# A graph layer on one core: own features one node range per pass, the neighbour product moved ahead of the sum, paced table copies, and 17 output blocks inside the last lane

## The chip, the core and the metric

The kernel runs on one core of a Trainium2 chip. The metric is the device time of one execution in microseconds. The engines are named as the profile names them: PE (TensorE, the matrix products; PEld is its weight load), DVE (VectorE), ACT (ScalarE), POOL (GpSimd) and SP (SyncE, which here only issues DMAs). Each engine runs its own queue in order; ACT and POOL issue DMAs from theirs as well.

## What is computed

There are V = 100,000 nodes with C = 64 features and E = 3.3 million edges (both directions of 1.6 million random pairs, and one loop for each node), sorted by target:

```python
h = jnp.maximum(_layernorm(x, axis=-1), 0.0)
local, nbr = h[dst], h[src]
y   = concat([local, nbr - local], -1) @ W.T + b          # per edge
s   = segment_sum(y, dst); cnt = segment_sum(1, dst)
out = x + where(cnt > 0, s / max(cnt, 1), 0)
```

The mean over a node's edges of `y` is the node's own part, `h @ (W1 - W2) + b`, plus the mean of its neighbours' `h` times `W2`. So the edge work is a sum of neighbours' rows for each target and a count.

## The kernel before

The features are padded to R = 100,352 rows, 784 for each of 128 partitions, and handled in blocks of T = 28 rows a partition, 28 blocks in all.

**Preparing** (lines 260 to 404). For each block, `center` loads x and subtracts the mean, the variance is taken from ACT's squares, and the normalized rows are split into three bf16 parts on ACT and GpSimd (L390 to L395), which are written as `h3` (L396): 3 x 64 columns and a one for the count. `own_part` turns the rows with PE (L338), adds `b` by a product of ones with three bf16 parts of `b` (L360), multiplies by `w_own` (L361) and writes `hb`. `step_own` places its units of 8 rows between the other steps.

**Sorting the first two lanes** (L1272 to L1296). Edges are cut into 384 windows of 8128, four of them to a quad, 32 quads to a lane, three lanes. A window spans fewer than 256 target nodes. `sort_lane` sorts the keys of 128 windows, one on each partition, by source: merge steps of one ACT copy (L603) and two DVE minimum and maximum operations (L597, L598), then counts that find where each of 157 source columns of 640 nodes begins (L686 on ACT, L743 on DVE). Beside it run 1400 gathers of the edges left over (`chunks`, L513), the clearing of `acc`, and 157 copies of `h3` into `tables` (L1286), one in each step from the 40th, issued by ACT.

**The lanes** (`quads`, from L939). A lane runs seven passes over its 32 quads; pass x covers the source columns from `FROM[x]` to `FROM[x + 1]` (16, five times 24, then the rest). For one column of one quad, a pick, six products of one-hot `gh` with a table column give the rows of the sources (L1102), ACT casts them (L1105), and row-tiled products over 32 rows with the one-hot `dh` add them to the quad's 4 x 256 targets in `total` (L1116). At the end of a quad's columns, `clear` adds `total` to the sums of earlier passes (L1152), which `load_sums` fetched from `part_d` (L1030), and stores them again (L1164). `whole`, the tile for that, has one buffer.

In pass 1 (`OWN`), the loops are treated apart, since their source is the target itself: `selfs` counts them (L1135, L1155), `load_sums` loads the own rows of all four windows (`own`, L1036), and `add_own` adds count times own row by eight DVE operations a quad (L1172). The store of the sums is put off until these have run.

Work in the background of the picks is called from the loop at L1310: `rest` at 0.055 a pick (`fill_lane`, which spreads a lane's sorted keys with gathers L830 and L920), and `sorting` at `SORT` = 0.135 a pick, which sorts the third lane in lane 0 and 1, but not in pass 1 and pass 6. `pinned` ties the DVE operations of such work to their place; others go when their data allow it. DMA requests on SP go in order, so a request that waits holds back the next, the loads of `srs` (L984) among them, from which `gh` is made.

In the last pass, `close` makes sums of 65 columns and `finish` stores them to `acc`; each window's last row may be shared with the next and goes to `shared`.

**The end** (from L1324). Four indirect adds bring `shared` into `acc` (L1349), flags decide whether a slow path has to run (loops with 0 turns otherwise), and 28 blocks are put out: mean of `acc` (L1431), turned (L1441), copied (L1443), multiplied by `w_mean` (L1447), added to `hb * min(cnt, 1) + x` from GpSimd (L1434, L1435, L1448) and stored (L1449).

Of the kernel before, what the change touches and what calls it, by code (L numbers as in the profile page):

```python
# [28 lines left out]
P = 128  # L29
P = 128  # L30
# [42 lines left out]
SORT = 0.135  # L73
# [10 lines left out]
SUB = 8  # L84
GP = 8
# [7 lines left out]
def rows_of(v):  # L93


    return -(-(v + 2 * P) // (P * SUB)) * P * SUB

# [14 lines left out]
def gnn_preln(ctx: ExitStack, tc, x, src_w, dst_w, src_p, dst_p, src_a, dst_a, wT, b, out, V, E):  # L112
# [45 lines left out]
    assert NE - FROM[-2] > 2 * GP and NSG > 1 and NTB - FROM[-2] // TG >= SEG // TG  # L158
# [22 lines left out]
    part_d = dram.tile([SETS, P, W, NT * CE], F32, name="part_d")  # L181
# [12 lines left out]
    w_mean = consts.tile([P, 2, C], F32, name="w_mean")  # L194
    w_own = consts.tile([P, 2, C], F32, name="w_own")
    nc.vector.memset(w_mean, 0.0)
    nc.vector.memset(w_own, 0.0)
    for i in range(2):
        nc.sync.dma_start(w_own[i * C:i * C + C, i], wT[:C])
        nc.sync.dma_start(w_mean[i * C:i * C + C, i], wT[C:])  # L200
    nc.vector.tensor_sub(w_own, w_own, w_mean)
# [9 lines left out]
    turns = consts.tile([1, 2], I32, name="turns")  # L211
# [10 lines left out]
    b3 = consts.tile([3 * 32, 2, C], BF16, name="b3")  # L222
    nc.vector.memset(b3, 0.0)
    b_part = consts.tile([P, C], BF16, name="b_part")
    for i in range(3):
        nc.vector.tensor_copy(b_part, b_sb)
        nc.vector.tensor_sub(b_sb, b_sb, b_part)
        nc.vector.tensor_copy(b3[32 * i:32 * i + 1], b_part[32 * i:32 * i + 1, None, :].to_broadcast([1, 2, C]))
    ones3 = consts.tile([3 * 32, P], BF16, name="ones3")
    nc.vector.memset(ones3, 1.0)  # L230

# [4 lines left out]
    out_v = out.rearrange("(p t) c -> p t c", p=P)  # L236
# [23 lines left out]
    with tc.tile_pool(name="pre", bufs=2) as pre, tc.tile_pool(name="small", bufs=4) as small, \  # L260
            tc.tile_pool(name="pre_ps", bufs=1, space=PSUM) as pre_ps, \
# [24 lines left out]
        def bounds(m):  # L286
            n = min(P, NCH - m * P)
            d = pre.tile([P, CHUNK], I32, name="d")
# [12 lines left out]
            l_ps = pre_ps.tile([NMT, 2, P], F32, name="l_ps")  # L301
# [29 lines left out]
        normal, made = {}, {}  # L331

        def own_part():

            def turn(t, u):
                t_ps = own_ps.tile([P, SUB // 2, P], F32, name="t_ps")
                for i in range(min(SUB, T - u) // 2):
                    nc.tensor.transpose(t_ps[:, i], normal[t][:, u + 2 * i:u + 2 * i + 2].rearrange("p a c -> p (a c)"), ident)  # L338
                return t_ps

            def finish(t, u, o_ps):
                if u == 0:
                    made[t] = pre.tile([P, T, C], F32, name="own", bufs=2)
                n = min(SUB, T - u)
                nc.scalar.copy(made[t][:, u:u + n], o_ps[:, :n])
# [5 lines left out]
            yield  # L351
            behind = None
            for at, (t, u) in enumerate(units):
# [3 lines left out]
                o_ps = own_ps.tile([P, SUB, C], F32, name="o_ps")  # L357
                o2 = o_ps.rearrange("p (i a) c -> p i (a c)", a=2)
                for i in range(n // 2):
                    nc.tensor.matmul(o2[:, i], lhsT=ones3, rhs=b3.rearrange("p a c -> p (a c)"), start=True, stop=False)  # L360
                    nc.tensor.matmul(o2[:, i], lhsT=hT[:, i], rhs=w_own.rearrange("p a c -> p (a c)"),  # L361
                                     start=False, stop=True)
                if behind is not None:
                    finish(*behind)
                if at + 1 < len(units):
                    t_ps = turn(*units[at + 1])
                behind = t, u, o_ps
                yield
            finish(*behind)
# [3 lines left out]
        def step_own(t):  # L373
            if t > 0:
                next(owns)

        center(0)
        for t in range(0, NPT, T):
            center(t + T)
            step_own(t)  # L380
# [3 lines left out]
            step_own(t)  # L384
# [3 lines left out]
            parts = pre.tile([P, T, CT], BF16, name="parts", bufs=3)  # L388
            nc.gpsimd.memset(parts[:, :, C3:], 1.0)
            nc.scalar.copy(parts[:, :, :C], xt)  # L390
            step_own(t)
# [1099 lines left out]
```

## Time and profile before

| what | us |
|---|---|
| median of 3 runs | 16983.4 (16947.2 to 16985.4) |
| profiled execution | 16993.9 |
| its span, first to last instruction | 16991.8 |
| mean granted clock of PE | 0.913 |

The page gives busy time for each engine, groups of instructions by line with count, busy time, the mean of one in ns, and the idle time ahead of them with what ended it. A windows view gives, for each stretch, its length, the busy time of PE, PEld, DVE, ACT and POOL with the number of instructions in brackets, the granted clock, the share of the 16 DMA engines in use and GB/s. A timeline gives start, length and instruction.

### The profile page before, as it was taken

What the parts mean: (1) busy time and instruction counts of PE and PEld (TensorE: products, weight loads), DVE (VectorE), ACT (ScalarE), POOL (GpSimd) and SP (SyncE); (2) the same over time, 40 slices, a digit from 0 to 9 for tenths busy, and PEclk for the clock granted to TensorE, in tenths of its full rate; (3) what the DMA queues carried; (4) which work ended last, traced back from release to release, by engine and by line L of the source; (5) the groups of instructions that cost most, each with busy time, mean ns of one, the idle gap of its engine ahead of it and who ended that gap; (6) DMA issues with size and microseconds to landing.
All of it is one profiled execution on the core that took longest, in us unless ns stands there. A gap on an engine that the chain in (4) does not pass through costs nothing. (4 is left out here: it accounts for less than half of the span.)

```text
span 16991.8 us, 762352 instructions
## 1 busy us (share of the span) xinstructions
PE 14218.4 (84%) x343411; PEld 13316.3 (78%) x343411; DVE 13850.5 (82%) x18981; ACT 8698.5 (51%) x17939; POOL 2232.9 (13%) x2043
## 2 busy tenths in 40 slices
PE   6111117999998999999999889999999989999996
PEld 5000007999997999999899889999998889999995
DVE  6787998889998889988899877779778766666784
ACT  5233346545554555565455645555554545555542
POOL 5565660000001000100000000001000000000015
PEclk7555558999999999999999999999999999999998
DMA  6962224555554455545555445555455544545557
GB/s 255 147 72 53 38 47 137 169 166 170 173 161 144 153 164 166 143 150 166 164 172 171 138 153 156 175 167 143 153 165 163 168 148 154 169 155 169 160 139 263
DMA packets 1939346, 2600.22 MB, mean 153 GB/s; under 512 B 955944, under 2 KB 1622454, under 8 KB 1931030
## 3 DMA queue, kind: packets, MB, share of 16 engines
q1 hardware_dynamic: 1765580, 2386.78, 44.6%
q0 software_dynamic: 62304, 99.25, 3.4%
q10 hardware_dynamic: 108188, 65.39, 3.0%
q8 instruction: 2684, 43.97, 1.1%
q14 instruction: 590, 4.83, 0.1%
HBM read 1898.80 MB, written 690.78 MB: 152 GB/s over the span
## 5 line engine op out<-in xcount | busy, mean ns | idle before, releaser
L1105 ACT CAST gs<-gp 128x386 bf16<-128x386 f32 x15072 | 6877.6, 486 | 5655.4 <-PE gp L1102 5234.1
L1102 PE MATMUL gp<-tab,gh 128*128 128x193 bf16 x90432 | 8118.3, 248 | 205.8 <-ACT gs L1105 110.2
L1102 PEld LDWEIGHTS <-gh 128*128 128x128 bf16 x90432 | 7612.0, 98 | 565.7 <-issue 526.4
L1116 PE MATMUL total<-gs,dh 32*128 32x193 bf16 x241152 | 5538.2, 243 | 297.2 <-issue 235.2
L1050 DVE TENSOR_SCALAR gh<-srs,pcols 128x2048 bf16<-128x2048 int16 (+1 forms) x5760 | 3954.5, 739 | 2155.6 <-PE gp L1102 1901.8
L1116 PEld LDWEIGHTS <-dh 32*128 32x128 bf16 x248832 | 5120.6, 93 | 744.8 <-issue 664.6
L470 DVE TENSOR_TENSOR dh<-dt,column 128x2048 bf16<-128x2048 int16 (+1 forms) x3840 | 4503.9, 1199 | 159.7 <-remote 97.5
L603 ACT COPY tmp<-keys 128x512 f32<-128x512 f32 (+16 forms) x1347 | 1092.0, 813 | 1852.8 <-DVE keys L598 974.7
L522 PE MATMUL gp<-nb,hot 128*128 128x193 bf16 x1400 | 279.5, 359 | 1924.2 <-DVE sums L533 794.5
L522 PEld LDWEIGHTS <-hot 128*128 128x128 bf16 x1400 | 180.2, 138 | 2023.3 <-DVE sums L533 819.2
L513 POOL DMA_INDIRECT nb<-h,si x1400 | 1329.6, 950 | 836.9 <-issue 387.6
L597 DVE TENSOR_TENSOR keys<-tmp,keys 128x512 f32<-128x512 f32 (+16 forms) x1347 | 1212.3, 916 | 141.2 <-ACT tmp L603 79.3
L598 DVE TENSOR_TENSOR keys<-tmp,keys 128x512 f32<-128x512 f32 (+16 forms) x1347 | 1216.8, 917 | 29.5 <-remote 6.6
L830 POOL DMA_INDIRECT kf<-ksort,at_i x123 | 136.4, 1109 | 7969.3 <-DVE keys L819 6467.6
L1152 DVE TENSOR_TENSOR whole<-total,whole 128x1544 f32<-128x1544 f32 x576 | 1013.8, 1760 | 107.2 <-PE total L1116 106.4
L1019 POOL DMA_INDIRECT rows_x<-h,xs x192 | 203.7, 1061 | 4038.2 <-PE gp L1102 2448.8
L814 DVE COPY_PREDICATED moved<-bits,moved 128x762 int32<-128x762 int32 (+1 forms) x420 | 294.0, 700 | 2.8 <-DVE keys L598 0.3
L920 POOL DMA_INDIRECT kx<-ksort,xat x144 | 140.7, 977 | 1117.6 <-DVE xat L916 607.9
L1172 DVE SCALAR_TENSOR_TENSOR whole<-own,whole 128x193 f32<-128x193 bf16 x768 | 267.7, 414 | 0.0
L1149 ACT COPY whole<-total 128x386 f32<-128x386 f32 x384 | 156.9, 497 | 204.5 <-PE total L1116 152.1
L686 ACT ACTIVATE junk<-keys,bound 128x536 bf16<-128x536 f32 (+2 forms) x280 | 197.0, 704 | 76.8 <-remote 37.4
L361 PEld LDWEIGHTS o_ps<-w_own,hT 128*128 128x128 f32 x784 | 156.5, 248 | 84.6 <-ACT hT L356 46.4
(209 smaller groups left out, 4056.5 us busy)
## 6 DMA issues: line engine op xcount, KB each, us to landing
srs<-sr_d SPq DMA_DIRECT2D x1824, 512.0 KB
part_d<-whole SPq DMA_DIRECT2D x2304, 193.0 KB
whole<-part_d SPq DMA_DIRECT2D x2304, 193.0 KB
tab<-tables SPq DMA_DIRECT2D x471, 242.5 KB
tables<-h ACTq DMA_DIRECT2D x157, 242.5 KB
h<-parts SPq DMA_DIRECT2D x28, 1358.0 KB
own<-h SPq DMA_DIRECT2D x384, 97.0 KB
srs<-sr_d SPq DMA_DIRECT2D x96, 320.0 KB
```

The lines of the kernel that those rows point to most:

```text
L470: return nc.vector.tensor_tensor(out.rearrange("p k (a d) -> p k a d", d=D), numbers[:, :, None].to_broadcast(shape), turned[n].rearrange( ...
L513: last[POOL] = nc.gpsimd.indirect_dma_start(out=nb[:, j], out_offset=None, in_=h3, in_offset=bass.IndirectOffsetOnAxis(ap=si[:, u, at:at + ...
L522: last[PE] = nc.tensor.matmul(ps[:, :CE], lhsT=before[0][:, i], rhs=before[1][:, i, :CE], start=before[2] == 0 and i == 0, stop=before[2] ...
L597: nc.vector.tensor_tensor(lo, tmp, hi, ALU.min)
L598: last[DVE] = nc.vector.tensor_tensor(hi, tmp, hi, ALU.max)
L603: last[ACT] = nc.scalar.copy(tmp, lo)
L814: nc.vector.copy_predicated(moved[:, :n, :, :w], mask.to_broadcast(shape), src)
L1050: nc.vector.tensor_scalar(gh[:, b, :n].rearrange("p c i s -> p (c i s)"), srs[q, s // SL][:, :n].rearrange("p c i s -> p (c i s)"), pcols[ ...
L1102: last[PE] = nc.tensor.matmul(gp[:, i], lhsT=ghots[q, s][:, b, i], rhs=row[:, b + i * (NB - NR), :CE], start=b == 0, stop=b == NR - 1)
L1105: last[ACT] = nc.scalar.copy(gs[q, s], gp)
L1116: nc.tensor.matmul(total[:, i, to(b)], lhsT=hot[at, b * P:b * P + P], rhs=of[at], start=flags.get("start", False) and b == 0, stop=flags.g ...
L1152: last["hots"] = last[DVE] = nc.vector.tensor_tensor(whole[:, :, :NT * CE], total[:, :, :NT * CE], whole[:, :, :NT * CE], ALU.add)
```

## The change

1. **The product with W2 moves ahead of the sum.** `w_own` and `w_mean` become one `w_cat`, and each pair of rows gets two products over 64 rows instead of a bias product and one over 128. One half of the result, with `b` added by DVE, goes to `hb`; the other, `hp`, is split into the bf16 parts of `h3`, now two blocks behind (`split`). The output blocks need no product any more.

```diff
-                    nc.tensor.matmul(o2[:, i], lhsT=ones3, rhs=b3.rearrange("p a c -> p (a c)"), start=True, stop=False)
-                    nc.tensor.matmul(o2[:, i], lhsT=hT[:, i], rhs=w_own.rearrange("p a c -> p (a c)"),
-                                     start=False, stop=True)
+                    for a in range(2):
+                        k = slice(a * C, a * C + C)
+                        nc.tensor.matmul(o_ps[:, a, i].rearrange("p s c -> p (s c)"), lhsT=hT[k, i],
+                                         rhs=w_cat[k].rearrange("p s c -> p (s c)"), start=True, stop=True)
...
-                nc.scalar.copy(made[t][:, u:u + n], o_ps[:, :n])
+                nc.scalar.copy(turned_h[t][:, rows].rearrange("p (i a) c -> p i a c", a=2), o_v[:, :, :, 1])
+                nc.vector.tensor_tensor(made[t][:, rows].rearrange("p (i a) c -> p i a c", a=2), o_v[:, :, :, 0],
+                                        b_sb[:, None, None, :].to_broadcast([P, n // 2, 2, C]), ALU.add)
...
+        def split(t):
+            hp = turned_h.pop(t)
+            parts = pre.tile([P, T, CT], BF16, name="parts", bufs=3)
+            nc.gpsimd.memset(parts[:, :, C3:], 1.0)
+            nc.scalar.copy(parts[:, :, :C], hp)
+            yield
+            nc.gpsimd.tensor_tensor(hp, hp, parts[:, :, :C], ALU.subtract)
+            nc.scalar.copy(parts[:, :, C:2 * C], hp)
+            yield
+            nc.gpsimd.tensor_tensor(parts[:, :, 2 * C:C3], hp, parts[:, :, C:2 * C], ALU.subtract)
+            nc.sync.dma_start(h3_v[:, t:t + T], parts)
```

2. **Own rows by pass.** Passes 1 to 4 each load the own rows of one of a quad's four windows and add them; the counts are carried with the sums in `part_d`.

```diff
-                if x == OWN:
-                    owns[q] = own = load.tile([P, W, NT, CT], BF16, name="own", bufs=1)
-                    for i in range(W):
...
+                if OWN <= x < OWN + W:
+                    owns[q] = own = load.tile([P, NT, CT], BF16, name="own", bufs=1)
+                    w = q * W + x - OWN
...
-            def add_own(q, whole):
+            def add_own(q, i, whole):
                 own = owns.pop(q)
-                for i in range(W):
-                    for b in range(NT):
...
+                for b in range(NT):
+                    part = whole[:, i, b * CE:b * CE + CE]
+                    later_on(KEPT + b, lambda b=b, part=part: nc.vector.scalar_tensor_tensor(
+                        part, own[:, b, :CE], whole[:, i, NT * CE + b:NT * CE + b + 1], part, op0=ALU.mult, op1=ALU.add))
```

3. **Paces.** The copies into `tables` go with every third step; the sorting of the third lane goes at 0.11 a pick in all passes but the last, and one counting step gets a `yield`.

```diff
-SORT = 0.135
+SORT = 0.11
...
-                    k = i - 40
-                    if 0 <= k < NCB:
+                    k, r = divmod(i - 40, 3)
+                    if r == 0 and 0 <= k < NCB:
...
-                sorted_ += SORT * (x not in (OWN, NSG - 1))
+                sorted_ += SORT * (x < NSG - 1)
```

4. **Output inside lane 2.** From pass 2 of the last lane, the sorting's tiles are given back and each pick takes a step of `finish_rows`: two of the four indirect adds, then 17 blocks (`DONE`), which lane 0 and 1 have completed, in quarters of 7 rows a partition (`TQ`), with the arithmetic on GpSimd.

```diff
+            for k in range(DONE):
+                for u in range(0, T, TQ):
+                    of = slice(u, u + TQ)
+                    at, ht, xo = (post.tile([P, TQ, w], F32, name=name) for name, w in (("at", C1), ("ht", C), ("xo", C)))
+                    nc.sync.dma_start(at, acc_k[k][:, of])
+                    yield
+                    nc.sync.dma_start(ht, hb_k[k][:, of])
+                    yield
+                    nc.sync.dma_start(xo, x_k[k][:, of])
+                    for _ in range(3):
+                        yield
+                    cnt = post.tile([P, 3, TQ], F32, name="cnt")
+                    nc.vector.tensor_scalar_max(cnt[:, 0], at[:, :, C], 1.0)
+                    nc.vector.reciprocal(cnt[:, 1], cnt[:, 0])
+                    nc.vector.tensor_scalar_min(cnt[:, 2], at[:, :, C], 1.0)
+                    nc.gpsimd.tensor_tensor(ht, ht, cnt[:, 2, :, None].to_broadcast([P, TQ, C]), ALU.mult)
+                    nc.gpsimd.tensor_tensor(ht, ht, xo, ALU.add)
+                    yield
+                    nc.gpsimd.tensor_tensor(xo, at[:, :, :C], cnt[:, 1, :, None].to_broadcast([P, TQ, C]), ALU.mult)
+                    nc.gpsimd.tensor_tensor(ht, ht, xo, ALU.add)
+                    for _ in range(3):
+                        yield
+                    nc.sync.dma_start(out_k[k][:, of], ht)
+                    yield
...
             for l, x in quads():
+                if l == NL - 1 and x > OWN:
...
+                    with pinned(last["hots"].ins):
+                        next(finishing, None)
```

5. **The end.** Eleven blocks remain, each by `rows_out`: counts on DVE, `hb * min(cnt, 1) + x` on GpSimd, mean and sum on DVE. A new loop, `again`, repeats the 17 blocks if the flags or the windows' bases say that lane 2 or the slow path touches them; its number of turns, 0 or 17, is worked out beside the other flags. A block is now 3584 rows in a row, 28 to a partition.

```diff
+        mean = pool.tile([P, T, C], F32, name="mean")
+        nc.vector.tensor_mul(mean, at[:, :, :C], cnt[:, 1, :, None].to_broadcast([P, T, C]))
+        nc.vector.tensor_add(mean, mean, ht)
+        nc.sync.dma_start(to, mean)
...
+        load_all(DONE)
+        load_all(DONE + 1)
+        for k in range(DONE, NBK):
+            load_all(k + 2)
+            rows_out(post, post_ps.tile([P, 2, T], F32, name="cnt"), loads.pop(k), out_k[k])
```

More of the change, by code (lines that the diff above doesn't have):

```diff
@@ L84 @@
 SUB = 8
+TQ = 7
 GP = 8
@@ L96, in rows_of, with drain @@
     return -(-(v + 2 * P) // (P * SUB)) * P * SUB
+def drain(events):
+    for _ in events:
+        pass
 def nodes_per_step(npt):
@@ L235, in gnn_preln @@
     acc_v = acc.rearrange("(p t) c -> p t c", p=P)
-    out_v = out.rearrange("(p t) c -> p t c", p=P)
+    KR = P * T
+    NBK = R // KR
+    AHEAD_W = sum(QUADS[:-1]) * W
+    DONE = int(AHEAD_W * EW / E * V * 0.99) // KR
+    assert R == NBK * KR and T % TQ == 0 and AHEAD_W % P == 0 and 0 < DONE < NBK
+    x_k, hb_k, acc_k, out_k = (of.rearrange("(k p t) c -> k p t c", p=P, t=T) for of in (x, hb, acc, out))
     sorts = ctx.enter_context(ExitStack())
@@ L383, in gnn_preln @@
             nc.scalar.activation(st[:, 3], st[:, 2], AF.Sqrt, bias=eps, scale=1.0 / C)
-            step_own(t)
+            splits = split(t - 2 * T) if t > T else iter(())
+            next(splits, None)
+            step_own(t, 1)
             nc.vector.reciprocal(st[:, 4], st[:, 3])
@@ L387, in gnn_preln @@
             normal[t] = xt
[L388 to L391, printed above, removed]
[L392 to L396 removed]
+            step_own(t, 1)
+            next(splits, None)
+            step_own(t, -(-T // SUB) - 3)
+            drain(splits)
             if 0 < t // T <= NMT:
@@ L402, in gnn_preln @@
             bounds(m)
-        for _ in owns:
-            pass
+        next(owns)
+        drain(split(NPT - 2 * T))
+        drain(owns)
+        drain(split(NPT - T))
     with ExitStack() as early:
@@ L1216, in quads @@
                     half_hots(g + 1, 0)
[L1217 to L1218 removed]
+                for _ in picks(g + 1):
+                    yield groups[g + 1][:2]
                     count[0] += 1
@@ new lines, in gnn_preln @@
+    with tc.tile_pool(name="again", bufs=2) as again, tc.tile_pool(name="again_ps", bufs=2, space=PSUM) as again_ps:
+        with tc.For_i(0, n_again, 1) as c:
+            sets = tuple(again.tile([P, T, w], F32, name=name) for name, w in (("at", C1), ("ht", C), ("xo", C)))
+            for tile_, of in zip(sets, (acc_k, hb_k, x_k)):
+                nc.sync.dma_start(tile_, of[ds(c, 1)].rearrange("o p t c -> (o p) t c"))
+            rows_out(again, again_ps.tile([P, 2, T], F32, name="cnt"), sets,
+                     out_k[ds(c, 1)].rearrange("o p t c -> (o p) t c"))
```

179 lines of the change are left out of this document (82 added, 97 removed).

## The prediction

> **What bounds the kernel now.** I read the page first, for the span and the slices of 425 us.
>
> ```profile
> span 16991.8 us, 762352 instructions
> ...
> PE   6111117999998999999999889999999989999996
> ...
> DVE  6787998889998889988899877779778766666784
> ```
>
> Four stages show. One slice prepares features; five sort two lanes (PE 1, DVE 7 to 9); then PE stands at 9 for 14 ms; the last slice falls off. Next comes the table of windows, cut at the ends of passes (by the last L1152 of a pass), then at the other stages.
>
> ```profile
> core 0: us, PE busy (x) PEld busy (x) DVE busy (x) ACT busy (x) POOL busy (x), PEclk, DMA share, GB/s
> 3115.00:3855.00 740.00, 702.74 (x18953) 669.51 (x18951) 644.73 (x971) 366.94 (x781) 11.48 (x10) 0.99 0.57 172
> 3855.00:4549.00 694.00, 675.66 (x16877) 639.90 (x16876) 651.24 (x873) 410.61 (x878) 8.67 (x8) 1.00 0.53 167
> ...
> 13243.00:13989.00 746.00, 684.22 (x16866) 643.88 (x16866) 517.09 (x688) 358.39 (x766) 45.38 (x48) 0.95 0.48 151
> 13989.00:14669.00 680.00, 672.87 (x16892) 639.11 (x16890) 472.13 (x520) 358.21 (x769) 0.00 (x0) 1.00 0.51 163
> ```
>
> The rows are pass 1 and 2 of lane 0 (pass 2 with sorting), then pass 2 and 3 of lane 2. PE bounds a plain pass: 673 of 680 us. Nothing in the change takes a matmul out of the passes, so the passes can only win their PE idle time: 37 us in pass 1 of lane 0, 62 in pass 2 of lane 2, 7 in pass 3.
>
> ```profile
> 45.00:385.00 340.00, 233.28 (x1459) 204.52 (x1458) 210.87 (x158) 226.29 (x312) 182.19 (x77) 0.76 0.66 239
> 564.00:1043.00 479.00, 56.55 (x280) 35.85 (x280) 383.42 (x409) 156.26 (x157) 267.18 (x284) 0.50 1.16 111
> 1050.00:1400.00 350.00, 53.12 (x259) 32.74 (x257) 340.05 (x362) 140.97 (x143) 233.88 (x248) 0.50 0.20 37
> 16690.00:16980.00 290.00, 187.84 (x1107) 170.26 (x1106) 129.14 (x212) 52.11 (x104) 189.57 (x53) 0.81 0.86 333
> ```
>
> Preparing: no engine over 70%, so chains between engines. Sorting: DVE at 97% (340 of 350) when alone, at 80% while the tables are copied and DMA stands at 1.16. Output: DMA at 0.86, and nothing of the passes left beside it.
>
> **The tail, the largest term.**
>
> ```profile
> 16635.04 1.77 DVE L1152 TENSOR_TENSOR whole<-total,whole 128x1544 f32<-128x1544 f32 x1 [2.96 <-PE total L1116]
> ...
> 16674.48 0.35 SPq L1420 DMA_DIRECT2D at<-acc  x1
> ...
> 16678.83 0.21 DVE L1428 TENSOR_SCALAR cnt<-at 128x28 f32<-128x28 f32 x1 [7.87 <-DMA at<-acc]
> ...
> 16693.22 0.35 SPq L1449 DMA_DIRECT2D out<-yt  x1
> ...
> 16965.61 21.98 SPq L1449 DMA_DIRECT2D out<-yt  x3
> ```
>
> The timeline gives 317 us from the first load (16674.5) to the end: 18.7 to the first store, then 25 periods to the third last, (16965.6 - 16693.2)/25 = 10.9 us a block. What ends a period:
>
> ```profile
> POOL ht L1434 <- DVE some L1433: 98.4, 26, 4.8
> DVE yt L1448 <- POOL ht L1435: 109.2, 22, 5.0
> ```
> ```profile
> L1435 POOL TENSOR_TENSOR ht<-ht,xo 128x1792 f32<-128x1792 f32 x28 | 111.4, 3979 | 2.2
> ...
> L1434 POOL TENSOR_TENSOR ht<-ht,some 128x1792 f32<-128x1792 f32 x28 | 89.3, 3190 | 113.9 <-DVE some L1433 100.0 <-DMA ht<-hb 13.9
> ...
> L1349 POOL DMA_INDIRECT acc<-some,at x4 | 6.2, 1549 | 12.3 <-DMA some<-shared 6.6 <-DMA acc<-some,at 5.7
> ```
> ```profile
> L1431 DVE TENSOR_TENSOR mean<-at,cnt 128x1792 f32<-128x1792 f32 x28 | 56.6, 2020 | 0.9
> ```
>
> GpSimd's 3.2 + 4.0 = 7.2 us, then VectorE's sum, then the next block's counts. The transposes, copies and products of L1441 to L1448 go, but 7.2 + 2.0 (the new sum, as L1431) + some 0.7 for counts is still 9.9. So I take 10.2 us a block (bounds 9 and 10.9). Eleven blocks remain: 16 + 10 x 10.2 + 4.3 (a landing as at 16678.8) = 122 us for 317, or -195. Two of four indirect adds go, 1.55 + 1.9 us each: -7. A third skipped loop costs a few us: the 39 us between L1152's last start and the first load hold two such loops beside much else. **Tail -200** (-185 to -215).
>
> **Table copies.** All 157 are issued by ACT between 564 and 1043 us.
>
> ```profile
> L1286 ACTq DMA_DIRECT2D tables<-h x157: 559/2803/5240, 564.2 to 1042.9; - x157
> ```
> ```profile
> L597 DVE TENSOR_TENSOR keys<-tmp,keys 128x1024 f32<-128x1024 f32 x258 | 311.5, 1228 | 56.0 <-ACT tmp L603 24.5 <-ACT junk L686 22.4 <-issue 8.5
> ```
>
> One issue takes 0.56 at the least and 2.8 us in the median, a full queue holding ACT, and VectorE waits for ACT's copies. One copy in three steps spreads them over 471 steps. The stretch's 383 us of DVE at the 97% of the next one is 395 us, so 84 us could go. A copy's DMA share, 1.16 - 0.20, spread over three times the steps leaves about 0.5: no longer full. I give 10 back for copies now beside the counting at the lane's end. **-75** (-95 to -20).
>
> **Preparing.** The transposes stay; 392 bias products go; each product with the own weights becomes two over half the rows, giving own and mean part together. ACT's copies stay in number, GpSimd's work too; VectorE gets 112 sums from PSUM with b.
>
> ```profile
> L361 PE MATMUL o_ps<-w_own,hT 128*128 128x128 f32 x784 | 186.5, 372 | 26.9 <-ACT hT L356 26.4
> ...
> L360 PE MATMUL o_ps<-b,ones 96*128 96x128 bf16 x392 | 101.3, 259 | 40.6 <-ACT own L345 34.6 <-DVE b L228 5.9
> ...
> L1448 DVE TENSOR_TENSOR yt<-y_ps,ht 128x512 f32<-128x512 f32 x84 | 56.1, 689 | 171.9 <-POOL ht L1435 125.2 <-PE y_ps L1447 46.2
> ```
> ```profile
> L1102 PE MATMUL gp<-tab,gh 128*128 128x193 bf16 x90432 | 8118.3, 248 | 205.8 <-ACT gs L1105 110.2
> ...
> L1116 PE MATMUL total<-gs,dh 32*128 32x193 bf16 x241152 | 5538.2, 243 | 297.2 <-issue 235.2
> ```
>
> Products over a quarter of the rows run side by side here: 23 ns each (5538/241152) against 90 of L1102. If halves do too, PE loses 101 us; if not, it gains 186 - 101 and binds. The 84 wide sums at 0.69 (28 narrower besides) are 60 to 70 us of DVE, which then is at some 80%. I take -10 for a shorter chain, and +15 because the split now runs two blocks late and is drained at the end (two GpSimd operations of 3.5 us for each of two blocks). **+5** (-45 to +75).
>
> **Own features and sorting.** Pass 1 holds 256 L1172 a lane; the change leaves 64 there and puts 64 in each of passes 2 to 4. Loads of own rows move with them. Sorting now also runs in pass 1, at 0.11 for 0.135 a column.
>
> ```profile
> SPq L1164 <- DVE whole L1172: 105.7, 95, 5.6
> SPq L1039 <- DMA own<-h: 71.1, 31, 3.3
> ```
> ```profile
> DVE gh L1050 <- DMA srs<-sr_d: 41.7, 19, 4.4
> ```
> ```profile
> L1172 DVE SCALAR_TENSOR_TENSOR whole<-own,whole 128x193 f32<-128x193 bf16 x768 | 267.7, 414 | 0.0
> ...
> L597 DVE TENSOR_TENSOR keys<-tmp,keys 128x512 f32<-128x512 f32 x330 | 226.3, 690 | 0.0
> ```
>
> In pass 1 SP waits with the stores of sums, behind it the srs loads, and gh waits for those. Per quad, DVE loses 6 x 0.41 = 2.5 us there and gets 2.6 sorting steps of 1.4 = 3.7: 645 + 39 = 684 of 740, no more than pass 2's 94%. So about 15 of the 37 idle us go, in three lanes, less 10 for tighter DVE: **-35** (-100 to +40).
>
> **Seventeen blocks inside lane 2.** 692 picks (one column of one quad each) of the 768 in pass 2 carry 68 units of a quarter block: 272 GpSimd operations of 448 elements, a quarter of L1434 and L1435, so 3.6 us a unit (4.2 with fixed parts), 245 to 285 in all; 204 small DVE operations, some 30 us (0.15 each, an estimate from L1428 at 0.21 for four times the elements); 272 DMAs of a block's 333 GB/s x 10.9 us = 3.6 MB, 62 MB in 613 us (680/768 x 692), 100 GB/s on 163, a DMA share of 0.8 if it grows in step. Room: DVE idles 208 of 680. In program order a unit has ten picks, 8.9 us; its store stands on SP at the ninth, and srs, dt and sums loads queue behind it. xo is issued at 1.8, so the store waits if landing takes over 8.0 - 1.8 - 3.6 = 2.6 us; the large load of the tail took 4.3. A wait of 2 us is inside the lead of srs, a group of 8 picks, 7 us. On POOL, lane 2's kf and kx gathers queue between the units; they are wanted a pass later.
>
> ```profile
> PEld L1116 <- issue: 66.8, 59, 3.4
> ```
> ```profile
> L513 POOL DMA_INDIRECT nb<-h,si x1400 | 1329.6, 950 | 836.9 <-issue 387.6 <-PE gp L522 179.5 <-remote 137.8
> ...
> L830 POOL DMA_INDIRECT kf<-ksort,at_i x123 | 136.4, 1109 | 7969.3 <-DVE keys L819 6467.6 <-DVE o L849 1034.9 <-DVE at_i L771 331.5
> ```
>
> This pass already loses 66 us (746 - 680) in a burst of 48 kx gathers, in which PE waits for "issue" (13500 to 13750). More DMA may repeat that; the units on the same queue may also thin the burst out. No row has GpSimd arithmetic beside the passes' VectorE work. Bounds: 0, all covered, and +150, turns (below) plus a burst's loss. The nearest row is GpSimd's gather issue, 1.11 us in the passes for 0.95 in the sort, 17%: I take **+45**. By the Trainium skill, SBUF — State Buffer, "Who interferes with whom", a VectorE operation with two SBUF inputs or in a two-port mode and a GpSimd operation reading SBUF exclude each other ("the other fully blocks"); by it this term would be about +110.
>
> Costed at nothing: two count columns more in the 386 of the carried sums, on DMA at 0.5; one buffer for the transposes' PSUM tile, since the next transposes stand behind products that already wait for its copy; one for `d`, filled once; a few more DVE operations of one element ahead of the loops. If the cover were gone each would be a few us.
>
> **Sum**: -200 - 75 + 5 - 35 + 45 = -260. 16993.9 (the profiled execution, 2.1 outside its span) gives 16734; the median of the runs shown is 10.5 lower, so **16723 us**.
>
> **Rivals.**
> 1. GpSimd and VectorE take turns in lane 2's pass 2: 425 (472 x 692/768) + 30 + 245 to 285 = 700 to 740 us for 613, +90 to +130 instead of +45: 16770 to 16810. For it: gh and dh fill most of DVE's time. Against: the 17% above. It is the Trainium skill's rule named above; chance 0.25.
> 2. Preparing becomes PE-bound, halves one after another (+75), and the copies only move their cost (-20): 16850. Against: L1116. Chance 0.08.
> 3. **Slower**: SP stands at each unit's store until its GpSimd work ends, and srs loads come late by all of it. Price: what a unit takes beyond its 8.9 us, 68 times. Without this term the change is worth 305 us, so it decides at 4.5 us, a unit of 13.4; that asks for landings of 2.6, the lead of 7 and 4.5, 14 us. At a unit of 15 us: 6.1 x 68 = +415 instead of +45, 17093. In the tail, at a DMA share of 0.86, a load four times as large lands in 4.3; 0.03.
> 4. The change undone at run time: the loop "again" repeats the 17 blocks, +185: 16910. The slow path's lines have no instruction here, so the flags were clean; 0.02.
> 5. The forecast, or better by the passes and the first stage: 0.62.
>
> Faster by over 0.3% (51 us, about what a measurement can tell): 0.93; within: 0.04; slower: 0.03. Range 16580 to 16880: below, 140 us of the terms' lower ends, which hardly all meet; above, rivals 1 and 2.
>
> **What would show it.** Stores of out 10 us apart for eleven blocks and 160 us behind the last L1152; VectorE near 95% from 564 us on; the first sort beginning at 390 to 410; pass 1 at 720 to 735; lane 2's pass 2 at 740 to 800. A pass 2 over 900 would make it wrong, so would a preparing stage over 450.

## The result, and the profile after

The changed kernel takes **16854.56 us** (median of 4 runs, 16846.39 to 16868.46) against 16965.29 (4 runs) for the kernel before on the same chip: a ratio of 0.9931 [0.9918, 0.9944], 111 us less. 16723 was predicted, 260 less. The direction was right, the gain less than half of it, and the time lies within the stated range of 16580 to 16880.

The profiled execution took 16861.5 us for 16993.9 before, 132 less. Cut at the first merge step of the sort, the first copy of a sum in lane 0, the ends of passes 1 and 2 of lane 2, its last L1167 (L1152 before) and the end of the span, the two traces differ like this:

| stage | before | after | difference | predicted |
|---|---|---|---|---|
| start to first merge step (preparing) | 503.2 | 585.9 | +83 | +5 |
| to the first copy of a sum (sorting, tables) | 2146 | 2092 | -54 | -75 |
| lanes without pass 2 of lane 2 | 13241 | 13170 | -71 | -35 |
| pass 2 of lane 2 | 745 | 860 | +115 | +45 |
| tail | 357 | 152 | -204 | -200 |
| sum | 16992 | 16860 | -132 | -260 |

Two terms, preparing and pass 2 of lane 2, miss by 78 and 70 us, which is more than the 128 that are missing in the sum. The slices of the page of after show both:

```profile
span 16859.8 us, 762019 instructions
...
PE   6111116999999899999999799999999979999996
DVE  7797998899999788988998777779878887777686
...
POOL 4565661000000100100000100001000350000002
```

POOL's 3 and 5 in slices 32 and 33 of 421 us are the 17 blocks inside lane 2, and PE falls to 7 in the second of them. The windows of after (us, then busy time of PE, PEld, DVE, ACT and POOL, granted clock, DMA share, GB/s) are cut at the ends of its own stages:

```profile
45.00:470.00 425.00, 282.37 (x1891) 218.06 (x1891) 281.88 (x268) 243.79 (x322) 195.37 (x81) 0.66 0.53 195
650.00:1100.00 450.00, 65.18 (x310) 39.02 (x309) 424.55 (x465) 178.09 (x182) 299.06 (x318) 0.50 0.44 71
3140.00:3877.00 737.00, 701.76 (x18946) 667.90 (x18944) 684.24 (x993) 399.92 (x851) 13.04 (x15) 0.99 0.52 162
...
13207.00:14066.00 859.00, 722.95 (x16869) 672.88 (x16866) 733.66 (x947) 360.46 (x769) 382.52 (x320) 0.91 0.66 205
14066.00:14743.00 677.00, 673.77 (x16927) 641.70 (x16920) 493.63 (x585) 360.36 (x772) 0.00 (x0) 1.00 0.54 169
16710.00:16860.00 150.00, 0.37 (x1) 0.08 (x1) 59.55 (x88) 0.00 (x0) 83.06 (x25) 0.51 0.70 274
```

By these windows preparing is 85 us longer, and still no engine is busy for over 70% of it. While the tables are copied, DVE now stands at 94% (424.55 of 450) where it had 80. Pass 1 of lane 0 takes 737 us, of which DVE fills 684, as worked out. Pass 2 of lane 2 has PE idle for 136 of 859 us, and pass 3 right behind it for 3 of 677.

The timeline of the tail in after:

```profile
16759.60 0.35 SPq L1494 DMA_DIRECT2D out<-mean  x1
...
16769.16 0.35 SPq L1494 DMA_DIRECT2D out<-mean  x1
...
16836.11 19.47 SPq L1494 DMA_DIRECT2D out<-mean  x3
```

From 16759.60 to 16836.11 are eight periods, 9.56 us a block for 10.2 predicted. In the issues of the table copies (minimum, median and longest in ns, first and last start in us) the median is back at the least value, and the copies reach to 1786 us:

```profile
L1339 ACTq DMA_DIRECT2D tables<-h x157: 558/559/5331, 645.6 to 1786.5; - x157
```

The stalls of ACT are not all gone. Thirty of the copies fall into the counting at the first lane's end, where the steps are short, and there an issue takes 3 us in the median:

```profile
L1339 ACTq DMA_DIRECT2D tables<-h x30: 559/2977/5331, 1504.4 to 1647.4; - x30
```

**Preparing.** The last store of `h3` is issued at 471.0 us; before, it was at 384.7. The groups of lines and the waits (us in total, times, longest) of after between 45 and 470 us ("issue" in such lines is time in which the engine waits for nothing that the profile shows, "remote" a wait that it puts down to another core or an unknown queue):

```profile
L362 PE MATMUL o_ps<-w_cat,hT 64*128 64x128 f32 x1512 | 186.1, 413 | 122.7 <-ACT hT L357 122.7
```
```profile
PE o_ps L362 <- ACT hT L357: 122.7, 106, 4.5
...
POOL parts L385 <- DMA h<-parts: 103.5, 19, 7.0
POOL hp L388 <- ACT parts L386: 102.5, 19, 28.8
```

1512 of the 1568 products over 64 rows are busy for 186.1 us, as long as 784 over 128 rows before (186.5), so halves do run side by side. PE is not the bound; it waits 123 us for ACT's copies `hT`. And GpSimd stands 104 us at a memset, where it stood 6 before. The timeline, for one unit of rows and one such memset (start, length, instruction, and in brackets the idle time before it and what ended it):

```profile
263.18 0.33 SPq L392 DMA_DIRECT2D h<-parts  x1
...
264.99 1.11 PE L335 MATMUL t_ps<-ident,xt 128*128 128x128 f32 x4
266.20 0.59 ACT L357 COPY hT<-t_ps 128x512 f32<-128x512 f32 x1 [0.82 <-PE t_ps L335]
...
267.45 2.08 PE L362 MATMUL o_ps<-w_cat,hT 64*128 64x128 f32 x16
268.89 0.15 POOL L385 MEMSET parts<- 128x56 bf16 x1 [5.74 <-DMA h<-parts]
```

Transposes, copy and products go in turns, one unit at a time. The memset of the ones column for block k + 3 stands in GpSimd's queue right behind its last work for block k, so it waits for block k's store to land, 5.7 us, and GpSimd's subtractions for the next block stand behind it. (A store has landed when the profile shows its transfer complete.)

**Pass 2 of lane 2.** The groups of after in that pass, by shape (busy us, mean ns, idle before):

```profile
L1065 DVE TENSOR_SCALAR gh<-srs,pcols 128x2048 bf16<-128x2048 int16 x288 | 324.1, 1175 | 60.5 <-PE gp L1117 41.4 <-DMA srs<-sr_d 19.1
L486 DVE TENSOR_TENSOR dh<-dt,column 128x2048 bf16<-128x2048 int16 x192 | 262.9, 1393 | 62.3 <-remote 58.5 <-PE total L1131 3.8
L1309 POOL TENSOR_TENSOR ht<-ht,xo 128x448 f32<-128x448 f32 x68 | 97.1, 1428 | 5.2
L1306 POOL TENSOR_TENSOR ht<-ht,xo 128x448 f32<-128x448 f32 x68 | 90.3, 1328 | 5.3
L1308 POOL TENSOR_TENSOR xo<-at,cnt 128x448 f32<-128x448 f32 x68 | 81.3, 1195 | 5.3
L1305 POOL TENSOR_TENSOR ht<-ht,cnt 128x448 f32<-128x448 f32 x68 | 66.6, 979 | 468.6 <-DVE cnt L1304 434.6 <-DMA srs<-sr_d 17.5 <-DMA whole<-part_d 7.5
```

A unit's GpSimd work is 4.93 us, 335 in all, where 245 to 285 were taken. `gh` takes 1.175 us; without units (`fin_none`, below) it takes 0.749. `dh` takes 1.393 for 1.217. That is 288 x 0.426 + 192 x 0.176 = 156 us more on VectorE. SP waits as well (13207 to 13860 us), at the load of `ht` for the landing of an earlier store, at the store for GpSimd, and at the load of `at` for GpSimd:

```profile
SPq L1296 <- DMA out<-ht: 91.6, 37, 4.8
...
SPq L1312 <- POOL ht L1309: 91.0, 47, 38.0
...
SPq L1294 <- POOL xo L1308: 74.1, 34, 16.9
```

### The profile page after: what moved, and what is told of

Read it like the earlier page. It is cut to its first block, busy times and chain, and to the rows that moved or that the text cites. A ratio compares the mean times of both kernels' runs of the same rounds, so it can differ in the third digit from the quotient of the medians.

```text
span 16859.8 us, 762019 instructions
## 1 busy us (share of the span) xinstructions
PE 14074.2 (83%) x342627; PEld 13148.5 (78%) x342627; DVE 14008.1 (83%) x19118; ACT 8657.8 (51%) x17827; POOL 2446.4 (15%) x2281
## 5 line engine op out<-in xcount | busy, mean ns | idle before, releaser
L1131 PE MATMUL total<-gs,dh 32*128 32x193 bf16 x241152 | 5552.8, 243 | 286.7 <-issue 193.6
L1065 DVE TENSOR_SCALAR gh<-srs,pcols 128x2048 bf16<-128x2048 int16 (+1 forms) x5760 | 4080.0, 760 | 2012.8 <-PE gp L1117 1867.3
L1131 PEld LDWEIGHTS <-dh 32*128 32x128 bf16 x248832 | 5136.3, 93 | 703.2 <-issue 592.7
L1167 DVE TENSOR_TENSOR whole<-total,whole 128x1544 f32<-128x1544 f32 x576 | 1012.8, 1758 | 73.5 <-remote 62.9
L362 PE MATMUL o_ps<-w_cat,hT 64*128 64x128 f32 x1568 | 193.7, 414 | 124.0 <-ACT hT L357 124.0
L362 PEld LDWEIGHTS o_ps<-w_cat,hT 64*128 64x128 f32 x1568 | 162.4, 300 | 166.0 <-ACT hT L357 164.8
```

The costliest lines, as they stand in the source:

```text
L362: nc.tensor.matmul(o_ps[:, a, i].rearrange("p s c -> p (s c)"), lhsT=hT[k, i], rhs=w_cat[k].rearrange("p s c -> p (s c)"), start=True, sto ...
L1065: nc.vector.tensor_scalar(gh[:, b, :n].rearrange("p c i s -> p (c i s)"), srs[q, s // SL][:, :n].rearrange("p c i s -> p (c i s)"), pcols[ ...
L1131: nc.tensor.matmul(total[:, i, to(b)], lhsT=hot[at, b * P:b * P + P], rhs=of[at], start=flags.get("start", False) and b == 0, stop=flags.g ...
L1167: last["hots"] = last[DVE] = nc.vector.tensor_tensor(whole[:, :, :NT * CE], total[:, :, :NT * CE], whole[:, :, :NT * CE], ALU.add)
```

## The experiments

Chips differ: the kernel before took 16957 to 16983 us on the chips of the first runs, of the pair above and of `after_again`, `fin_dma`, `fin_pool` and `fin_slow`, and 16543 to 16567 on those of the other experiments. A whole time is compared with that of before on the same chip, and stages are compared on chips of one kind. All but the pair, `best_slow` and `best_all` are single runs. Four of them put all 28 blocks out at the end besides what is left in lane 2, so that their whole times say nothing about the pass: `fin_dma` 17094.66 and `fin_pool` 16987.36 (before 16956.63), `fin_dma_tied` 16594.06 (16551.99) and `dma_late` 16660.94 (16558.94). The changed kernel again gave 16843.15 (before 16956.63) and 16492.4 (before 16551.99).

> The changed kernel as it is, beside the next three on the same chip. Pass 2 of lane 2 at 835-865 us, mean gh operation of VectorE there about 1.2 us for 0.75 in the next pass, last h3 store at 465-475 us. All theories expect this; it is the yardstick.

> The changed kernel as it is, the yardstick on this chip for the next three. Pass 2 of lane 2 at 835-865 us with all 17 blocks in it.

**1. What lengthens preparing.** The theory was the single buffer of the transposes' PSUM tile; its rival, ACT and the split.

```diff
-                t_ps = own_ps.tile([P, SUB // 2, P], F32, name="t_ps", bufs=1)
+                t_ps = own_ps.tile([P, SUB // 2, P], F32, name="t_ps", bufs=2)
```

To make room, the two `st` tiles share a bank. `before_tps1` is the kernel before with one buffer.

> The changed kernel with two buffers for the transposes' PSUM tile instead of one (and the two halves of st in one PSUM tile, to make room). Theory A: the preparing stage grew from 385 to 471 us because with one buffer PE's transposes of the next unit wait for ACT's copy of this one, so PE and ACT take turns, 3.9 us a unit of 8 rows and 14.5 us a block. Then the period of the h3 stores falls from 14.5 to 12.5-13 us, the last h3 store to 410-425 us (the drain of two blocks stays), and the whole by 45-60 us. Rival B: the stage is slower because of VectorE's 112 new sums or the later split; then the period stays at 14-14.5 and the last store at 455-475. Rival C: the halves of the products cost PE more; then the period stays as well and PE's busy time is over 75% of the stage.

> The kernel before with one buffer for the transposes' PSUM tile instead of two, nothing else. Theory A (PE and ACT take turns): the period of the h3 stores rises from 12.7 to 14-15 us, the last store from 385 to 420-445, the whole by 35-60 us. Rivals B and C (VectorE's sums, the split, the halved products): within 8 us of the kernel before, last store at 380-395.

Two buffers in after bring the last store from 467 (`fin_none`, whose preparing is the changed one) to 444 us; one buffer in before takes it from 382 (`pace_only`, below) to 405. So the buffer is worth 23 us, not 85, and about half of what the theory expected (410 to 425 and 420 to 445); the rival's figures did not come about either. The whole times are 16488.11 and 16580.47, for 16566.68. The 23 us are not turns alone. PE's own operations are longer with one buffer, in `before_tps1` as in after: a transpose takes 374 and 417 ns for 325 in before, a product of L361 421 for 369 in before, at a granted clock of 0.66 in both for 0.76. With two buffers in after the clock is 0.70 and a transpose takes 348. No run separates the two. And in `tps2` another wait grew (45 to 400 us), from 93.9 in that window of after:

```profile
POOL parts L386 <- DMA h<-parts: 135.1, 24, 6.5
```

The next pair takes that wait away: three fixed tiles, their ones written once.

```diff
+        three = [pre.tile([P, T, CT], BF16, name=f"parts{i}", bufs=1) for i in range(3)]
+        for parts in three:
+            nc.gpsimd.memset(parts[:, :, C3:], 1.0)
...
-            parts = pre.tile([P, T, CT], BF16, name="parts", bufs=3)
-            nc.gpsimd.memset(parts[:, :, C3:], 1.0)
+            parts = three[t // T % 3]
```

> The changed kernel with the ones of the three h3 tiles written once ahead of the loop instead of by a memset in each block. Theory D: in the changed kernel GpSimd stands at the memset of the block three later, which is put right behind a block's last GpSimd operation and so waits 5-6 us in each block until the h3 store just issued has landed; the next subtraction, ACT's second cast and the products behind it come late by that. Then the period of the h3 stores falls from 15.0 to 12.5-13.7 us and the last store from 470 to 415-440. Rival A (only the single PSUM buffer, worth 23 us): the period stays over 14.5 and the last store over 460. Rival B (VectorE's sums): the same as A.

> The changed kernel with both: ones written once, and two PSUM buffers for the transposes. Theory D and A together: period 11.5-13 us, last h3 store at 385-415, first merge step at 490-525, the whole 50-80 us less than the changed kernel. Rival B (VectorE's 112 sums set the period): period still over 14, last store over 435.

Alone it gives 6 to 9 us: 461, for 467 in `fin_none` and 470 in `own_sort`, which ran on the same chip. Unchanged, the last store lay between 463 and 471 in all runs, and 415 to 440 was expected, so alone this looked like the rival. With two buffers the last store comes at 400: 67 us for both, where the parts alone give 23 and under 10. The whole times are 16496.01 and 16439.4, for 16543.48. The waits of `one_memset_tps2` have no memset in them, the granted clock is 0.75, and PE still waits for `hT`:

```profile
PE o_ps L363 <- ACT hT L358: 91.2, 32, 4.7
```

A block takes 12.7 us from store to store for 15.0 in after and 13.2 in before. What is left of the 85 is 400 - 382 = 18 us, near the 15 given to the two blocks' lag and its drain.

**2. The table copies alone.** Before, with `k, r = divmod(i - 40, 3)` and a copy where r is 0.

> The kernel before with the table copies at every third sorting step, nothing else. If the pacing is the cause of the 54 us by which the time from the first merge step to the first sum of pass 0 (2146 us before, 2092 in the changed kernel) is shorter, that time is 2080-2100 here and the whole 45-75 us less; DVE busy 93-97% between 564 and 1043 us. If the gain came from elsewhere, it stays over 2130.

Whole time 16523.13 against 16566.68, -44 us. From first merge to first sum it takes 1956 us, and 1996 in `before_tps1`, which has the old pace: -40.

**3. Pass 2 of lane 2.** First without units: the steps are left out and all 28 blocks are put out at the end.

> The changed kernel without the 17 blocks in lane 2: all 28 blocks are put out at the end. Pass 2 of lane 2, 860 us in the changed kernel and 745 before, gives the price of the blocks there: 740-755 if all of the 115 us are theirs, 800 or more if moving own rows and sorting had a part. The tail, 152 us in the changed kernel, grows by 17 blocks: at a period of 10 us by 170, to 320-330; so the whole is 55-70 us over the changed kernel.

16478.45 against 16566.68, -88: more than the -60 of the changed kernel on such a chip, where 55 to 70 us over the changed kernel were expected. The pass took 674 us for 848 with units (`after_third`), and the tail 314 for 151. **On these chips the 17 blocks inside the lane lost 174 us and saved 163.**

Then parts of the units: DMAs only, arithmetic only (the loads once ahead of the units, no stores), and everything at a quarter of the pace.

> Of the 17 blocks in lane 2 only the DMAs stay (three loads and a store for each unit, which stores hb as it is); the GpSimd and VectorE arithmetic for them is left out, and all 28 blocks are put out at the end. Theory A, GpSimd and VectorE exclude each other: pass 2 of lane 2 falls to 675-700 us, gh back to 0.75 us. Rival B, DMA traffic or requests waiting on SP: pass 2 stays at 780 or more. If both matter, 710-770.

> Of the 17 blocks in lane 2 only the arithmetic stays, 272 GpSimd and 204 VectorE operations on one block quarter loaded once, without loads and stores for each unit; all 28 blocks are put out at the end. Theory A (exclusion): pass 2 of lane 2 stays at 800-865 us, gh at 1.1-1.3 us. Rival B (DMA, SP): 675-720, gh at 0.75-0.85.

> The changed kernel with one step of the 17 blocks at every fourth pick instead of at every pick, so that they spread from pass 2 over 2768 picks into pass 5. Theory A: VectorE loses the same 200 us in all, but a quarter of it in each of four passes that have 200 us of idle VectorE: pass 2 at 685-710 us, passes 3 to 5 at 680-700, the whole 110-160 us less than the changed kernel on the same chip. Rival B, each blocked gh operation delays PE by itself, however spread: the four passes grow by 30-45 us each and the whole stays within 40 us.

`fin_dma` missed its question. With nothing between load and store, the DMAs were put ahead into pass 4 of lane 1 (829 us for 685, DMA at 265 to 274 GB/s in its first 250 us) and pass 0 of lane 2, and pass 2 went without, at 739. The arithmetic alone gave 840 us, against 852 for the whole on the same chip, and 745 (before) and 739 (`fin_dma`) without any. Groups of `fin_pool` in that pass:

```profile
L1065 DVE TENSOR_SCALAR gh<-srs,pcols 128x2048 bf16<-128x2048 int16 x288 | 323.8, 1174 | 42.2 <-PE gp L1117 41.5 <-DMA srs<-sr_d 0.5
L486 DVE TENSOR_TENSOR dh<-dt,column 128x2048 bf16<-128x2048 int16 x193 | 266.1, 1402 | 62.0 <-remote 55.9 <-PE total L1131 5.9
```

The same `gh` and `dh` as in after, with no DMA of a unit beside them. At a quarter of the pace (a step every fourth pick, so that units reach into pass 5) the pass took 761, passes 3 to 5 some 8 us more together, and the kernel 16774.43 for 16843.15, 69 us less. 110 to 160 less were expected by the first theory, under 40 by the second: the result lies between the two.

Next the DMAs alone, tied to their pick by three small VectorE operations for each unit, two of them copies into `ht`, and the arithmetic moved to VectorE.

```diff
-                    nc.gpsimd.tensor_tensor(ht, ht, cnt[:, 2, :, None].to_broadcast([P, TQ, C]), ALU.mult)
+                    nc.vector.tensor_tensor(ht, ht, cnt[:, 2, :, None].to_broadcast([P, TQ, C]), ALU.mult)
```

> As fin_dma, but each unit's loads and its store now hang on three small VectorE operations that stay in their place, so that the DMAs cannot run ahead as they did there; no GpSimd arithmetic, wrong values in those rows until the end writes all 28 blocks anew. Theory: GpSimd and VectorE exclude each other, and traffic costs little: pass 2 of lane 2 at 690-720 us (750-775 on a chip where the gathers of that pass cost their 65 us), gh at 0.75. Rival: 100 GB/s more traffic and SP's waits cost 40 us or more by themselves: 715 or more (780 or more).

> The changed kernel with the arithmetic of the 17 blocks on VectorE instead of GpSimd, at the same pace. VectorE then has some 580 us of its own in pass 2, 34 for the counts and 272 operations of 448 elements at about 0.5 to 0.55, 140 to 150: 755-765 us, which it cannot hide in 675. Theory (exclusion costs more than the work itself): pass 2 at 750-790, 60-100 less than with GpSimd, gh at 0.75. Rival (GpSimd saves VectorE time): 850 or more.

The DMAs alone took 780 us, which the rival gave, with `gh` untouched. Groups, then the waits of SP, in `fin_dma_tied`:

```profile
L1065 DVE TENSOR_SCALAR gh<-srs,pcols 128x2048 bf16<-128x2048 int16 x288 | 200.9, 750 | 225.8 <-DMA srs<-sr_d 149.4 <-PE gp L1117 72.1 <-PE total L1131 2.3
```
```profile
SPq L1296 <- DMA out<-ht: 199.3, 48, 6.4
```

The load of `ht` for a later unit is put into SP's queue right behind the store whose buffer it takes, SP stands there until the store has landed, and the loads of `srs` behind it come late: `gh` waits 149 us for them. `fin_dve` took 787, and the kernel 16433.45 for 16492.4. Its four additions and products a unit:

```profile
L1306 DVE TENSOR_TENSOR ht<-ht,xo 128x448 f32<-128x448 f32 x68 | 42.2, 621 | 1.7
L1309 DVE TENSOR_TENSOR ht<-ht,xo 128x448 f32<-128x448 f32 x68 | 42.2, 620 | 1.2
L1308 DVE TENSOR_TENSOR xo<-at,cnt 128x448 f32<-128x448 f32 x68 | 42.1, 619 | 0.9
L1305 DVE TENSOR_TENSOR ht<-ht,cnt 128x448 f32<-128x448 f32 x68 | 40.6, 597 | 0.0
```

That is 167 us of VectorE, against the 156 by which VectorE's own work stretches when GpSimd does it. Taking the arithmetic off VectorE saved VectorE next to nothing, and with GpSimd the pass is 61 us longer (848 for 787).

Last, is it the traffic or SP's standing at a load issued too early? A small VectorE write ahead of each load keeps it at its pick.

```diff
+                    nc.vector.memset(ht[:, 0, :1], 0.0)
                     nc.sync.dma_start(ht, hb_k[k][:, of])
```

> The arithmetic of the 17 blocks in lane 2 is left out (28 blocks at the end), their DMAs stay, and a small DVE write ahead of each load of a unit keeps that load at its pick, so that SP does not reach it while the store of an earlier unit is still landing. On the chip where before takes about 16550, pass 2 of lane 2 took 674 us without any units and 780 with the DMAs alone, in which SP stood 199 us at the load of ht behind the store's landing, with the loads of srs behind it. Theory A (SP standing at a load that was put in its queue too early costs the 106 us): pass 2 at 675 to 705, SP under 60 us at that load. Theory B (the 62 MB of traffic itself): pass 2 stays at 760 to 790. Where before takes about 16957, 65 us more for both.

> The changed kernel, with the same small DVE write ahead of each load of a unit; nothing is left out. On the chip where before takes about 16550 pass 2 of lane 2 took 848 us in the changed kernel and 674 without units. Theory A (waits on SP and turns of GpSimd and VectorE cost one beside the other): the waits on SP go and what the arithmetic costs by itself stays, 95 to 101 us in the run with the arithmetic alone: pass 2 at 765 to 790. Theory B (the turns of GpSimd and VectorE set the pass, and SP's waits lie beside them): 825 to 855, gh at 1.15 us or more. Where before takes about 16957: A 790 to 810, B 830 to 860.

Both theories fell in both runs: 838 us for the DMAs alone, 1032 for the whole. Waits of VectorE in `dma_late`, and of SP and VectorE in `after_late`:

```profile
DVE cnt L1305 <- DMA at<-acc: 131.0, 49, 7.9
DVE ht L1307 <- DMA xo<-in_x: 84.2, 39, 9.1
DVE ht L1306 <- DMA ht<-hb: 29.5, 33, 5.0
...
DVE gh L1065 <- DMA srs<-sr_d: 0.5, 1, 0.5
```
```profile
SPq L1315 <- POOL ht L1312: 333.1, 61, 37.3
```
```profile
DVE cnt L1305 <- DMA at<-acc: 279.7, 42, 43.8
```

The loads of `srs` are in time again, but now the unit's own loads aren't, and VectorE stands at the counts instead of SP at the load. So the two runs do not settle whether the traffic or SP's standing costs the 106 us; they show that a load put later is no cure. In `dma_late`'s timeline a load lands some 4 us after its issue:

```profile
13304.17 0.33 SPq L1295 DMA_DIRECT2D at<-acc  x1
...
13308.01 0.17 DVE L1305 TENSOR_SCALAR cnt<-at 128x7 f32<-128x7 f32 x1 [1.87 <-DMA at<-acc]
```

In `after_late` SP waits 333 us at the stores for GpSimd and the next loads stand behind them.

**4. Own rows and sorting.** After, with the old pace of sorting (0.135, none in pass 1).

> The changed kernel with the old pace of sorting: 0.135 a pick, none in pass 1 and pass 6. Own rows still go by pass. Theory: passes 1 were slow because SP stood at the stores of sums behind eight own additions and the srs loads came late; so pass 1 of all three lanes now takes 700-715 us like pass 1 of lane 2 in the changed kernel (708), and lane 0's pass 1, 737 in the changed kernel, has 25-35 us from sorting beside it. Rival: the own additions were never late and sorting is free, then pass 1 of lane 0 stays at 730-740.

Pass 1 takes 706, 702 and 704 us in the three lanes, for 746, 749 and 737 in `pace_only` and 724, 722 and 704 in `after_third`. So the spread own rows give 33 to 47 us a lane in pass 1, and sorting there takes some 20 back in the two lanes that sort. But it then has to be done elsewhere: pass 3 of lane 1 takes 761 for 719, while pass 2 takes 686 for 717. The whole, 16477.84 against 16543.48, is within 6 us of the gain of `after_third`.

**5. Together.** One memset, two buffers and a quarter of the pace (`best_slow`); the same with the old sort pace (`best_all`).

> All three mends together: ones written once, two PSUM buffers, and one step of the 17 blocks at every fourth pick. If the gains add up, 50-80 us in the first stage and some 69 us in lane 2 (as measured alone), 120-150 us less than the changed kernel, 1.4 to 1.6% less than the kernel before. If the first stage's gain is taken back by the sorting behind it, 80-100.

> best_slow with the old pace of sorting besides (0.135 a pick, none in pass 1 and pass 6). One look at that pace alone gave 25-38 us less between the first and the last sum than the changed kernel's pace. If that holds: 1.4-1.7% less than the kernel before. If it was noise: 1.15-1.35%, as best_slow.

16339.6 us against 16543.48, ratio 0.9874 [0.9858, 0.9891], and 16339.24 against 16551.99, 0.9872 [0.9856, 0.9889]: 1.3% less than before, where the changed kernel alone gives 0.4% on such a chip (16492.4 for 16551.99). The old sort pace adds nothing. Pass 2 of lane 2 and the tail in `best_all`:

```profile
12829.00:13554.00 725.00, 681.36 (x16921) 646.84 (x16919) 574.79 (x799) 364.35 (x778) 137.03 (x120) 0.98 0.58 181
16192.00:16341.00 149.00, 0.46 (x6) 0.08 (x1) 62.14 (x92) 0.00 (x0) 83.06 (x25) 0.52 0.70 276
```

## Why the prediction was right or wrong

**The tail (-200) was right**, -204, by its own steps: eleven blocks bound by GpSimd's two operations and VectorE's sum, 9.56 us each.

**The table copies (-75) gave -54.** The mechanism was right for the merge steps: ACT's issues fell from 2803 to 559 ns in the median, and VectorE rose to 94% (95 was expected). Counted from the first minimum or maximum of the sort (L597, L598 in before), the 300th comes 84 us earlier than before, the very 84 that were worked out, and the 660th still 80. The 720th, behind the counts at the first lane's end, comes only 52 earlier. So the step mis-sized is "10 back for copies now beside the counting": it is some 30. The counting itself takes 146 us for 116 before. ACT and VectorE in that window of after (1505 to 1651 us):

```profile
ACT junk L699 <- issue: 64.0, 25, 4.6
```
```profile
DVE pos L766 <- ACT junk L699: 74.5, 1, 74.5
```

One copy in three steps was paced by steps, and the steps of the counting are short: 30 copies come in 143 us, the DMA share is 0.88 for 0.23 before, an issue takes 2977 ns in the median, ACT's counts stand behind the issues, and VectorE waits 75 us for ACT's last count. The copies alone, in before, gave -40 on another chip, and there too the counting took longer, 134 us in `pace_only` for 103 in `before_tps1`.

**Preparing (+5) took +83, and here a step failed**: "one buffer for the transposes' PSUM tile, since the next transposes stand behind products that already wait for its copy", costed at nothing. With one buffer the transposes of the next unit can't run beside the copy of this one, PE, ACT and PE go in turns, and PE's operations are longer, at a granted clock of 0.66 for 0.76: 23 us alone, in either kernel. The prediction also said that GpSimd's work stays. Its instructions did; their place in the queue did not, and the memset that waits for a store's landing is a wait that the count of instructions can't show. Each of the two seems to cover the other, since only both together free 67 us. The two blocks' drain was about right (18 left). Rival 2, PE-bound halves, was false: 186.1 us for 1512 of them.

**Own rows and sorting (-35) gave -71.** Same sign, mis-sized: pass 1 gained 4, 24 and 41 us in the profiled pair, and the other passes 2 us together. Lane 2, where nothing is sorted, gained most; `own_sort` shows why, since the sorting in pass 1 costs the other two some 20 us each. Pass 2 of lane 1 took 29 more, and other passes gave that back.

**The 17 blocks (+45) took +115, and here a second step failed**: the value was chosen near a 17% loss of a gather's issue, and the disputed operations themselves lose 57% (`gh`) and 14% (`dh`). The mechanism is rival 1's. That +115 also lies within its price (+90 to +130) is in part luck. The price took the 472 us that VectorE works in pass 3; the row of pass 2 has 517, and with it the same sum gives 741 to 781 us for 613, +128 to +168. And the pair's pass before already held 57 us in which PE waits for "issue" at L1116 (55 at L1131 after). On the faster chips, where these waits are 2 to 4 us, the same term is +171 (677 in `pace_only`, 848 in `after_third`). Arithmetic alone gives 840 of 852 us on the chip where both ran, so there it is enough for most of the loss. That is what the Trainium skill, SBUF — State Buffer, "Who interferes with whom", says of a VectorE operation with two SBUF inputs or in a two-port mode and a GpSimd operation that reads SBUF, that each keeps the other out; the traces agree in that `gh` goes from 0.749 to 1.175 us with arithmetic beside it and stays at 0.750 with 62 MB of DMAs beside it. They do not show in which mode `gh` runs, and `dh`, the one with two inputs, lost much less.

But it isn't the only cause. "A wait of 2 us is inside the lead of srs" failed too. In `fin_dma_tied` `gh` waits 149 us for `srs`, in `after_third` 77, in the profiled after 19. The DMAs alone cost 106 us on the faster chips (674 to 780), VectorE's arithmetic 7 more, GpSimd's instead of it 61 more. A unit of ten picks is 8.9 us; a load's landing of about 4 us, 4.9 us of arithmetic and a store's landing don't fit, and what is next in line stands: SP, VectorE or GpSimd. How the +115 of the profiled pair divides between turns and landings stays open. Alone, each makes about 100, and together they don't add up; the DMAs alone were not measured on a chip of that pair's kind.

**Rival 3** came about only in part in the changed kernel, where SP stands 91 us at the stores for GpSimd and `gh` waits 19 us for `srs`. `after_late` shows the first half of its mechanism in full: SP at each store until GpSimd is done, the next loads behind it; what comes late there is the unit's own loads, and not `srs`. There a unit takes (13815.8 - 12874.0) / 67 = 14.1 us from store to store, beyond the 13.4 from which the rival was to decide, and the pass 358 us more than without units; the kernel, 16673.79 against 16558.94, is slower than before. In the changed kernel a load of `at` is issued 28 us (median) ahead of the counts that use it, in `after_late` 4.4.

```profile
L1315 SPq DMA_DIRECT2D out<-ht x68: 337/343/433, 12874.0 to 13815.8; - x68
```

**Rival 4**, the loop `again`, is out: the tail is 152 us, with no room for its 185.

## What to carry to other kernels

Count buffers as well as instructions: a tile's reuse puts a wait for a copy or for a store's landing into some engine's queue, two such waits can hide each other, and undoing one shows little. Pace by time and not by steps, where steps differ in length. Work moved "beside" a bound stage pays with the stage's slack: in a stage where VectorE has 21% left (533 of 674 us busy in `fin_none`), GpSimd arithmetic cost VectorE about as much as doing it there would, and loads and stores on the queue that feeds the stage cost 106 us alone. Spread such work thin (a quarter of the pace took 91 us off the pass and 69 off the kernel) before looking for another engine.

## What was not expected of the hardware

The same kernel before takes 2.5% more on some chips (16957 to 16983 us) than on others (16543 to 16567). By stages it is not the passes at large. Sorting took 2146 us there and, at the same pace, 1996 here (`before_tps1`). The lanes took 303 us more there, 182 of them in the three passes with a burst of 48 `kx` gathers (L920), 758, 800 and 745 us for 688, 756 and 677; the other eighteen passes differ by 1%. The burst's loss of 66 us, in which PE waits for "issue", is absent on the faster chips: waits of `pace_only` in pass 2 of lane 2, where before lost 66.8 at L1116 of PEld in that burst.

```profile
PEld L1116 <- issue: 20.4, 96, 2.8
...
PE gp L1102 <- issue: 3.7, 4, 1.7
```

So most of what was read as the kernel's own loss, the 62 idle us of this pass, is not there on the other chips; why chips differ stays open.
